# Layer 0's mix of a four-layer graph network: three passes over split operands in place of a recursive scheme of seven products

## The chip, the cores and the metric

The kernel runs on one core of a Trainium2 chip. The metric is the device time of one execution in microseconds (us); lower is better. A run reports the time of the whole execution; a profiled execution also reports the span from its first to its last recorded instruction, and the trace times every instruction within that span.

The engines of the core are TensorE (PE in the profile, with its weight loads listed apart as PEld), VectorE (DVE), ScalarE (ACT) and GpSimd (POOL). SyncE (SP) issues the DMAs. Matrix products are written by PE into PSUM, which is used in banks of 512 fp32 values for each of 128 partitions; the other engines read results from there.

## The reference

Input x has 32 batches of 512 nodes with 128 features; adj is a 512 x 512 matrix of non-negative weights. Four layers follow one another, each as x + layer(relu(layernorm(x))). Only layer 0 is changed:

```python
h0 = einsum('bnf,fg->bng', input, W[0])
h1 = einsum('bnf,fg->bng', input, W[1])
m = adj > 0
idx = cumsum(m.reshape(-1)) - 1
vals = e[0][idx].reshape(adj.shape)
A = softmax(where(m, vals, NEG), axis=1)
M = eye(N)
out = einsum('ij,bjg->big', A * M, h0) + einsum('ij,bjg->big', A * (1 - M), h1)
return out + bias
```

So each batch gets the off-diagonal attention times h1 (the mix, here written g), plus the diagonal of the attention times h0 (the own term), plus a bias. Layer 1 multiplies with adj and its square and projects with Theta; layer 2 passes messages through adj squared; layer 3 is an attention over the nodes. All inputs and outputs are fp32.

## The kernel before

**Tiling.** Nodes are cut into NT = 4 blocks of 128, batches into 16 pairs (index q, tiles of 128 x 4 x 2 x 128) and the pairs into 8 rounds of two (index r). All x stays on the chip from its load in layer 0 to its store at the end. A tile with nodes on the partitions serves the statistics and the mix; a projection needs features on the partitions, so each normalised tile h is turned into hT.

**Order.** PE, DVE, ACT and POOL run their instructions in the order in which the program writes them, and SP issues its DMAs in that order too. There is no scheduler: the order is written by hand with generators, where `next(steps)` emits the next part of a job and `go(steps, n)` its next n parts. Where an instruction waits, everything written behind it on the same engine waits as well.

**Start (up to L719).** The attention is made in four blocks of rows: exponentials, row sums, scaling by ACT (L677), then transposes by PE into the four banks `p_attT` (`transpose_rows`). ACT and DVE copy these banks into `attT` (`att_copies`, L346). `att_sums` (L348 to L366) lets DVE form three further sums s1, s2 and s4 of the four 256 x 256 quarters of attT. Meanwhile the first pairs are normalised, turned by PE (`pe_steps`, transposes in L307, for pairs 0 to 3) and projected.

**A pair before the mix.** `stats_steps` (L241 to L261) has DVE take BATCH_NORM_STATS2 over four stretches (L247), ACT the square root (L256), DVE a reciprocal (L258) and a shift `sh` (L259). `normed_steps` has ACT normalise with relu in eight instructions (L289). `turn_steps` (L320 to L335) turns a pair in two halves: DVE transposes blocks (L325), four DMAs write them to DRAM (L332) and one loads the turned tile (L334). `projected` (L458) multiplies by W[1] in 16 records of PE for a pair, `project_steps` (L472 to L484) has ACT copy the two banks to g (L483). `straight` (L733) lets POOL multiply hT with the attention's diagonal into hd, the left operand of the own term.

**The mix (`round0`, L804 to L958).** One round does two pairs by Strassen's scheme on 2 x 2 quarters: seven products in place of eight, in the order ORDER (L376 to L380). A left operand is a quarter of attT or a sum of quarters; a right operand is a part of g or one of four differences that POOL makes (`right_steps`, L368 to L374). `by_token` (L393 to L399, matmul in L397) does one product in four fp32 matmuls of 256 columns, each in two records. Products that share a result are accumulated in the banks a, c and d. `evict` (L824 to L844) has DVE add the banks into three tiles u or into x, and `add` (L850) has POOL add each u into x. The own term (`straight_block`, L801: four fp32 matmuls of 128 columns, eight records, for each call, four calls a round) is put in the banks as they end, and one bank of its own closes the round. The bias is added by POOL for the first quarter (`bias`, L466) and otherwise by the first eviction.

Between the products stand the other jobs of the round: turns of pairs 2r+2 and 2r+3, normalising two pairs on, statistics of pairs five ahead (`stats_a`, `stats_c`), statistics of the pairs whose layer 0 has ended (`own_a`, `own_c`, for layer 1), projections and right-hand differences of the next round, and the loads of x eight pairs on. From r = 3 on `late_parts` (L744 to L762) splits adj for layer 1. In round 0 the second half of the attention's transposes and copies stand inside the first products, and so do the transposes of adj for layer 1's square (`turn_adj`, L502 to L513).

**Layer 1** (from L960) is opened with `next(next_layer)` in the last round. Layers 1 to 3 use operands split in three parts (`PARTS`, high, low and mid; L424, L425) and matmuls of type fp32r for such products (`p_w`, L1010).

The order of the products, and the form of one:

```python
    ORDER = ((1, "a", True), (6, "c", True), (5, "d", True), (7, "c", False), (2, "a", False),
             (4, "c", False), (3, "d", False))
```

Of the kernel before, what the change touches and what calls it, by code (L numbers as in the profile page):

```python
# [17 lines left out]
P = 128  # L18
# [11 lines left out]
def kernel(  # L30
# [63 lines left out]
    def square_tile(name):  # L94
        return region0.tile([P, NT, N], F32, tag="square", name=name, bufs=2)
# [245 lines left out]
    sums = {}  # L341

    def att_copies(*which):

        for j, half, copy in which:
            copy(attT[:, j, half * H : half * H + H], pt[j][:, half * H : half * H + H])  # L346

    def att_sums():  # L348

        a11, a12 = attT[:, 0:2, 0:H], attT[:, 2:4, 0:H]  # L350
        a21, a22 = attT[:, 0:2, H:N], attT[:, 2:4, H:N]
        extra = region0.tile([P, 3, 2, H], F32, tag="sums", name="sums_att", bufs=1)
        s1, s2, s4 = extra[:, 0], extra[:, 1], extra[:, 2]
        sums["att"] = {1: a11, 2: a12, 3: s4, 4: a22, 5: s1, 6: s2, 7: a21}
        yield
        for out, p, bank_of, half, first in ((s1, a21, 2, 1, False), (s2, s1, 0, 0, False),
                                             (a21, a21, 0, 0, True), (s4, s2, 2, 0, True)):
            for k in range(2):
                b = pt[bank_of + k][:, half * H : half * H + H]
                if out is s1:  # L360
                    nc.vector.tensor_add(out[:, k], b, p[:, k])
                elif first:
                    nc.vector.tensor_sub(out[:, k], b, p[:, k])
                else:
                    nc.vector.tensor_sub(out[:, k], p[:, k], b)
            yield  # L366

    def right_steps(half, name, engs, right):  # L368
        b11, b12, b21, b22 = half(0, 0), half(0, 1), half(1, 0), half(1, 1)
        t = [region0.tile([P, 2, 2, D], F32, tag="rt", name=f"rt_{name}_{i}", bufs=6) for i in range(4)]  # L370
        right.update({1: b11, 2: b21, 3: b22, 4: t[3], 5: t[0], 6: t[1], 7: t[2]})
        for i, (p, q) in enumerate(((b12, b11), (b22, t[0]), (b22, b12), (b21, t[1]))):
            engs[i].tensor_sub(t[i], p, q)
            yield  # L374

    ORDER = ((1, "a", True), (6, "c", True), (5, "d", True), (7, "c", False), (2, "a", False),  # L376
             (4, "c", False), (3, "d", False))


    ORDER0 = (ORDER[0], ORDER[4]) + ORDER[1:4] + ORDER[5:]  # L380

    def products(name, form, left, right, evict, order=ORDER, on=lambda k, p: p):


        banks = {}
        for k, g, first in order:
            if first:
                banks[g] = bank(f"p_{name}_{g}")
            form(on(k, banks[g]), left[k], right[k], first)
            evict(k, banks[g])  # L390
            yield

    def by_token(p, a, b, first):  # L393

        for i in range(2):
            for k in range(2):
                nc.tensor.matmul(p[:, i * 2 * D : (i + 1) * 2 * D], a[:, k, blk(i)], b[:, k],  # L397
                                 start=(first and i == 0 and k == 0), stop=(k == 1),
                                 skip_group_check=True)  # L399

    def u_tile(name):
        return region0.tile([P, 2, H], F32, tag="u", name=f"u_{name}", bufs=3)
# [59 lines left out]
    def quad_tile(name):  # L462
        return region0.tile([P, 2, 2 * N], F32, tag="quad", name=name, bufs=2)


    def bias(r):  # L466
        x11 = xq[r][:, :, 0, 0:2, :]
        nc.gpsimd.tensor_add(x11, x11, b0[:, None, None, :].to_broadcast([P, 2, 2, D]))

    g, rights = {}, {}  # L470

    def project_steps(q, hT, copy=nc.scalar.copy):  # L472
        r, w = divmod(q, 2)
        if w == 0:
            if r % 3 == 2:
                g[r] = square_tile(f"g_{r}").rearrange("p t (b w f) -> p t b w f", b=2, w=2)
            else:
                t = quad_tile(f"g_{r}").rearrange("p w e -> p (w e)")
                g[r] = t.rearrange("p (t b w f) -> p t b w f", t=NT, b=2, w=2)
        pg = [projected(f"p_g_{q}_{b}", (at(hT, b), w0[:, 1, :])) for b in range(2)]  # L480
        yield
        for b in range(2):
            copy(g[r][:, :, b, w, :], pg[b])  # L483
            yield  # L484

    def right_of(r):
        rights[r] = {}
        return right_steps(lambda J, b: g[r][:, 2 * J : 2 * J + 2, b], f"g_{r}", [nc.gpsimd] * 4, rights[r])
# [84 lines left out]
    for i in range(3):  # L573
        eh = prep.tile([P, NK], BF16, name=f"eh_{i}")
        nc.gpsimd.tensor_copy(eh, ecoln)
        part = prep.tile([P, NK], F32, name=f"part_{i}")
        nc.gpsimd.tensor_copy(part, eh)
        if i < 2:
            nc.gpsimd.tensor_sub(ecoln, ecoln, part)
        parts.append(part)  # L580
    h = {q: normed_tile(q) for q in range(3)}
    hT = {q: feature_major(f"hT0_{q}") for q in range(4)}
# [26 lines left out]
    nc.vector.tensor_sub(rest, rows[:, :NK], pb[:, :, 0])  # L609
    def turn_first(b):  # L610
        p = bank(f"p_hT0_0_{b}")
        for t in range(NT):
            nc.tensor.transpose(p[:, blk(t)], h[0][:, b, t, :], ident)
        nc.scalar.copy(hT[0][:, :, b, :].rearrange("p b (a c) -> p b a c", c=QR), crossed(p))
# [10 lines left out]
    project = [project_steps(q, hT[q], c) for q, c in ((0, nc.scalar.copy), (1, nc.vector.tensor_copy))]  # L625
# [47 lines left out]
    def scaled_rows(t):  # L673
        if t == 0:
            nc.gpsimd.tensor_scalar(split(att[:, t, :]), crossed(us[t]), total[:, t : t + 1], None, OP.mult)
        else:
# [6 lines left out]
    attT = square_tile("attT")  # L683
# [4 lines left out]
    next(project[0])  # L688
# [10 lines left out]
    next(turned[1])  # L699
    scaled_rows(1)  # L700
# [5 lines left out]
    inverse(3)  # L706
    scaled_rows(3)
    next(project[1])
# [3 lines left out]
    go(project[1])  # L712
    left_of_att = att_sums()
    next(left_of_att)
    att_copies((0, 0, nc.scalar.copy), (1, 0, nc.vector.tensor_copy),
               (2, 0, nc.scalar.copy), (3, 0, nc.scalar.copy))
    go(early_stats_2, 3)
    next(squares)
    go(right_of(0))  # L719
# [59 lines left out]

    def projection(q):  # L780
        return project_steps(q, hT[f"hT0_{q}"] if q > 3 else hT[q])

    def diagonal_of(r, b):
        for q in (2 * r, 2 * r + 1):
            src = hT[f"hT0_{q}"] if q > 3 else hT[q]
            hd[q, b] = straight(src, b, adiag[0], f"hd_{q}_{b}")

    def x_block(r, I, b):
        return xq[r][:, :, b, 2 * I : 2 * I + 2, :]

    def of_pairs(ap):
        return ap.rearrange("p i (w f) -> p w i f", w=2)

    def halves(p):
        return p.rearrange("p (i e) -> p i e", i=2)

    def straight_block(p, src, I, weight, first):

        for i in range(2):
            for w in range(2):  # L800
                nc.tensor.matmul(p[:, (2 * i + w) * D : (2 * i + w + 1) * D], src(w)[:, blk(2 * I + i)], weight,  # L801
                                 start=(first and i == 0 and w == 0), stop=True, skip_group_check=True)

    def round0(r):  # L804

        now = rights.pop(r)
        if r == 0:

            adiag.append(region0.tile([P, N], F32, tag="rt", name="adiag", bufs=6))
            p_adiag = bank("p_adiag")
        A, C = 2 * r, 2 * r + 1

        def x_of(I, b):
            return x_block(r, I, b)

        def diagonal(p, I, b, first):
            straight_block(p, lambda w: hd[A + w, b], I, w0[:, 0, :], first)

        u = [u_tile(f"l0_{r}_{i}") for i in range(3)]
        held = {}

        def evict(k, p):  # L824
            pv = halves(p)
            if k == 1:
                nc.vector.tensor_add(tiles(u[0].rearrange("p i e -> p (i e)")), tiles(p), spread(b0, NT))
            elif k == 6:
                nc.vector.tensor_add(u[1], pv, u[0])
            elif k == 5:  # L830
                held["d"] = pv
            elif k == 7:
                nc.vector.tensor_add(u[2], pv, u[0])
                nc.vector.tensor_add(u[2], held["d"], u[2])
            elif k == 2 and r == 0:
                held["a"] = p
            elif k == 2:
                upper(p)
            elif k == 4:
                diagonal(p, 1, 0, False)  # L840
                nc.vector.tensor_add(x_of(1, 0), of_pairs(pv), x_of(1, 0))
            elif k == 3:
                diagonal(p, 0, 1, False)
                nc.vector.tensor_add(x_of(0, 1), of_pairs(pv), x_of(0, 1))  # L844
# [724 lines left out]
```

## Time and profile before

| what | value |
|---|---|
| median of 3 runs | 883.46 us (883.32 to 883.58) |
| profiled execution | 883.48 us |
| span of its trace | 881.7 us |
| instructions in the span | 15,654 |
| granted TensorE clock, 202.7 to 881.7 us | 1.00 |
| layer 0: first product starts | 28.96 us |
| layer 0: round 0 ends | 52.63 us |
| layer 0: rounds 1 to 6, each | 19.23 us |
| layer 0 ends, layer 1's first product follows | 183.6 us |
| PE busy from 202.7 to 881.7 us | 675.07 of 679.0 us |
| bytes moved by DMA | 102.81 MB |

How to read it: the times of day in the trace count from the start of the span. An engine's busy time leaves out issuing, branching and waiting on semaphores, but matmuls are pipelined with modelled ends, so a busy PE can hide short waits. The views used are the page's busy shares; the chain of waits, which follows the work that ended last back from step to step, each line with its start, its length, engine, tile and source line; the groups of instructions by line, with their count, mean duration and the idle time ahead of them; single instructions in a stretch of the timeline; and the windows, which give the busy time of each engine in a chosen stretch, with the count of its instructions behind it, then the granted clock, the DMAs' share and rate.

### The profile page before, as it was taken

The page shows a single profiled execution, that of the slowest core. Times are in us where ns is not written, and L with a number is a line of the kernel's source. Part 1 is how long each engine was busy: PE and PEld are TensorE (multiplying, and loading weights), DVE is VectorE, ACT ScalarE, POOL GpSimd, SP SyncE. Part 2 cuts the span into 40 slices and gives each one's busy share as a digit, 9 for nine tenths or more (in the row PEclk, how much of TensorE's full clock was granted, in tenths as well). Part 3 has the DMA queues.
Part 4 walks back from the last instruction along what each step waited for, and adds up shares of the span by engine and source line. Part 5 has one row for each costly group of instructions (what it writes and reads, how often), then busy time and mean ns, then how long its engine had stood idle before and what let it go on. Part 6 is the DMA issues. An engine that isn't in the chain of part 4 may idle for free.

```text
span 881.7 us, 15654 instructions
## 1 busy us (share of the span) xinstructions
PE 872.6 (99%) x5209; PEld 763.3 (87%) x5209; DVE 713.2 (81%) x1445; ACT 576.5 (65%) x1289; POOL 618.0 (70%) x599
## 2 busy tenths in 40 slices
PE   8999999999999999999999999999999999999998
PEld 4899999988888888888888888888889888899987
DVE  7888887568787787888689888888789789988875
ACT  5874554355556656556666888876688778766774
POOL 5876899986767877867586566565476766677664
PEclk9999999999999999999999999999999999999999
DMA  9166553131413113122242344455445555455433
GB/s 263 46 174 166 161 153 104 41 97 56 128 57 93 53 52 93 48 72 72 81 136 79 114 139 140 129 156 146 129 129 142 154 149 169 139 140 155 125 104 84
DMA packets 106960, 102.81 MB, mean 117 GB/s; under 512 B 9472, under 2 KB 93568, under 8 KB 106880
## 3 DMA queue, kind: packets, MB, share of 16 engines
q1 hardware_dynamic: 106592, 101.29, 41.0%
q8 instruction: 41, 0.67, 0.3%
q10 hardware_dynamic: 288, 0.52, 0.2%
q14 instruction: 39, 0.32, 0.1%
HBM read 52.50 MB, written 49.28 MB: 115 GB/s over the span
## 4 chain that ended last, share of the span: by engine, by line
PE 93%; POOL 3%; ACT 2%; DVE 1%; issue 1%; DMA 0%; POOLq 0%; ACTq 0%
PE p_av L1339 13%; PE p_l L1031 10%; PE p_hidden L1235 10%; PE p_score L1317 9%; PE p_x1T L409 9%; PE p_w L1010 5%; PE p_l_c L397 5%; PE p_l L458 3%; PE p_z L458 3%; PE p_l_a L397 3%; PE p_l_d L397 3%; PE p_g L458 3%; PE p_w L1012 3%; PE p_feat L1212 3%; PE p_hidden L1215 3%; PE p_query L1271 2%
## 5 line engine op out<-in xcount | busy, mean ns | idle before, releaser
L1339 PEld LDWEIGHTS p_av<-hv,ex 128*128 128x128 f32 x1024 | 119.1, 191 | 4.1 <-POOL hv L1301 1.1
L1339 PE MATMUL p_av<-hv,ex 128*128 128x129 f32 x1024 | 119.7, 274 | 0.8 <-POOL hv L1301 0.6
L289 ACT ACTIVATE h<-x,sh,rs 128x128 f32<-128x128 f32 x256 | 102.2, 483 | 11.9 <-DVE sh L259 11.0
L439 POOL TENSOR_TENSOR key<-key 128x512 fp32r<-128x512 f32 x32 | 48.1, 1503 | 83.9 <-DVE key L438 58.0
L1312 DVE TENSOR_TENSOR ex<-ex,adjTx 128x512 f32<-128x512 f32 x64 | 80.5, 1260 | 31.0 <-ACT ex L1310 29.2
L1312 POOL TENSOR_TENSOR ex<-ex,adjTx 128x512 f32<-128x512 f32 x64 | 99.6, 1573 | 6.9 <-issue 3.5
L1141 ACT ACTIVATE h<-x,sh,rs 128x128 f32<-128x128 f32 x256 | 102.9, 484 | 0.0
L247 DVE BATCH_NORM_STATS2 bn<-x 128x6 f32<-128x256 f32 x244 | 87.3, 417 | 0.0
L425 POOL TENSOR_TENSOR low_h<-h,high_h 128x512 fp32r<-128x512 f32 x32 | 54.5, 1704 | 45.9 <-PE p_w L1012 28.1
L1318 ACT ACTIVATE ex<-p_score 128x512 f32<-128x512 f32 x128 | 76.3, 598 | 11.5 <-PE p_score L1317 4.7
L1310 ACT ACTIVATE ex<-ex 128x512 f32<-128x512 f32 x128 | 77.3, 634 | 0.0
L1199 POOL TENSOR_SCALAR high_hT<-hT 128x512 fp32r<-128x512 f32 x32 | 20.5, 639 | 56.2 <-PE p_hidden L1215 28.8
L1255 POOL TENSOR_TENSOR x<-x,phi2b 128x256 f32<-128x256 f32 x64 | 56.2, 898 | 0.0
L425 POOL TENSOR_TENSOR low_hs<-hs,high_hs 128x512 fp32r<-128x512 f32 x32 | 44.4, 1399 | 13.2 <-ACT high_hs L424 12.9
L411 ACT COPY x1T<-p_x1T 128x512 f32<-128x512 f32 x32 | 18.7, 586 | 52.2 <-PE p_x1T L409 52.2
L1317 PE MATMUL p_score<-high_query,key 128*128 128x512 f32 x128 | 50.6, 395 | 0.0
L1317 PE MATMUL p_score<-low_query,key 128*128 128x512 f32 x128 | 50.5, 394 | 0.0
L1317 PE MATMUL p_score<-mid_query,key 128*128 128x512 f32 x128 | 50.4, 394 | 0.0
L443 ACT ACTIVATE high_query<-p_query 128x512 fp32r<-128x512 f32 x32 | 19.2, 601 | 47.5 <-PE p_query L1271 47.5
L256 ACT ACTIVATE sd<-bn,eps 128x8 f32<-128x8 f32 x46 | 14.0, 304 | 55.3 <-DVE bn L247 52.2
L1012 PE MATMUL p_w<-th,x1T 128*128 128x128 f32 x256 | 49.0, 272 | 0.0
L1150 DVE STREAM_TRANSPOSE hb<-h 128x512 f32<-128x512 f32 x64 | 43.6, 698 | 2.8 <-DMA d<-hb 2.6
(256 smaller groups left out, 2612.8 us busy)
## 6 DMA issues: line engine op xcount, KB each, us to landing
d<-hb SPq DMA_DIRECT2D x128, 128.0 KB, 2.4
hT<-d SPq DMA_DIRECT2D x32, 512.0 KB, 3.6
d_hT<-hb_hT SPq DMA_DIRECT2D x112, 128.0 KB, 2.4
hT<-d_hT SPq DMA_DIRECT2D x28, 512.0 KB, 3.3
x<-in_x_dram SPq DMA_DIRECT2D x32, 256.0 KB, 5.1
dv<-hvb SPq DMA_DIRECT2D x128, 64.0 KB, 1.9
hvt<-dv SPq DMA_DIRECT2D x32, 256.0 KB, 2.5
out_dram<-x SPq DMA_DIRECT2D x31, 256.0 KB, 2.5
```

The costliest lines, as they stand in the source:

```text
L247: nc.vector.bn_stats(st[:, k].rearrange("p e s -> p (e s)"), xt[q][:, b, t : t + 2, :].rearrange("p t f -> p f t"))
L289: nc.scalar.activation(h[:, b, t, :], xt[q][:, b, t, :], AF.Relu, bias=shift[q][:, i : i + 1], scale=scale[q][:, i : i + 1])
L397: nc.tensor.matmul(p[:, i * 2 * D : (i + 1) * 2 * D], a[:, k, blk(i)], b[:, k], start=(first and i == 0 and k == 0), stop=(k == 1), skip_g ...
L409: nc.tensor.matmul(p, right[part][:, blk(t)], left[part][:, t, :], start=(t == 0 and part == 0), stop=(t == NT - 1 and part == 2))
L425: nc.gpsimd.tensor_sub(low, x, high.bitcast(F32))
L458: nc.tensor.matmul(p[:, blk(t)], hT(t), w, start=(i == 0), stop=(i == len(terms) - 1))
L1031: nc.tensor.matmul(p, adj_parts[part][:, t, blk(i)], w[r][part][:, t, :], start=(part == 0 and t == 0), stop=(part == 2 and t == NT - 1))
L1141: nc.scalar.activation(h[:, t, :], xt[q][:, b, t, :], AF.Relu, bias=shift[q][:, i : i + 1], scale=scale[q][:, i : i + 1])
L1235: nc.tensor.matmul(sums2[n], weighed_features[n][i][:, blk(t)], sq[i][:, t, :], start=False, stop=(i == 2 and t == NT - 1), skip_group_che ...
L1312: eng.tensor_mul(split(ex[:, t, :]), split(ex[:, t, :]), crossed(mask[:, t, :]))
L1317: nc.tensor.matmul(p, keys[n][i][:, t, :], query[n][i], start=(i == 0), stop=(i == 2))
L1339: nc.tensor.matmul(po[:, i, : D + 1], ex[:, t, blk(i0 + i)], hv[:, t, :], start=(t == 0), stop=(t == NT - 1))
```

## The change

The recursive scheme goes, and with it the sums of the attention's quarters, the right-hand differences, the tiles u and the rounds of two pairs. In its place:

- The transposed attention is split from its PSUM banks into three fp32r tiles `att_high`, `att_low` and `att_mid`, in two halves: four scaled high parts, on ACT (for the first half two of them on DVE), then four low and four mid parts on DVE. There is no fp32 `attT`.
- g of each pair is split as it leaves PSUM: ACT makes the high part by a scaled copy, DVE the low part from the bank and the high part, POOL the mid part from the two. W[1] is scaled beforehand by a power of two, on POOL. For pair 0 `project_first` does it by way of a copy in SBUF, so that the banks come free.
- The mix of a pair is three passes (high, low, mid), each over two halves of the nodes: `mixed` makes one pass of one half with eight fp32r matmuls of 256 columns. The three passes accumulate in one bank for each half.
- The own term of a pair goes into the same two banks, ahead of the passes (for pair 0 behind them). One addition on DVE for each bank then brings it into x.
- The bias is added by POOL to the whole of x, two instructions a pair.
- The loop runs over single pairs, 1 to 15. A pair's order in it: own term, turn of pair q+3, normalising of q+4, statistics of q-1 for layer 1, projection and split of q+1, three passes of half 0, statistics of q+5, addition, three passes of half 1, addition.
- Pair 3 is turned by DVE and DMAs, not by PE. The transposes of adj move from the start to pairs 3 and 4, their DMAs to pair 5; the split of adj runs one part a pair from pair 6 on; layer 1 is opened in pair 14, and its next part stands in pair 15.

The core of the diff:

```diff
-        return region0.tile([P, NT, N], F32, tag="square", name=name, bufs=2)
+        return region0.tile([P, NT, N], F32, tag="square", name=name, bufs=1)
...
-    def att_sums():
...
-    def right_steps(half, name, engs, right):
...
-    def products(name, form, left, right, evict, order=ORDER, on=lambda k, p: p):
...
-    def by_token(p, a, b, first):
...
+    att_parts = [region0.tile([P, NT, N], F32R, name=f"att_{part}", bufs=1) for part in PARTS]
...
+    def att_high(j, half, on_act):
+
+        p, (high, low, mid) = of_half(j, half)
+        if on_act:
+            nc.scalar.activation(high, p, AF.Copy, scale=DOWN)
+        else:
+            nc.vector.tensor_scalar(high, p, DOWN, None, OP.mult)
+
+    def att_low(half):
+
+        for j in range(NT):
+            p, (high, low, mid) = of_half(j, half)
+            nc.vector.tensor_sub(low, p, high.bitcast(F32))
+
+    def att_mid(half):
+
+        for j in range(NT):
+            p, (high, low, mid) = of_half(j, half)
+            nc.vector.scalar_tensor_tensor(mid, p, 1.0 / UP, high.bitcast(F32), OP.mult, OP.subtract)
...
+    def bias(q):
+
+        for b in range(2):
+            nc.gpsimd.tensor_add(xt[q][:, b], xt[q][:, b], spread(b0, NT))
...
         pg = [projected(f"p_g_{q}_{b}", (at(hT, b), w0[:, 1, :])) for b in range(2)]
         yield
+        g_tiles(q)
         for b in range(2):
-            copy(g[r][:, :, b, w, :], pg[b])
+            high, low, mid = (part[:, :, b, :] for part in g[q])
+            nc.scalar.activation(high, pg[b], AF.Copy, scale=DOWN / LOW)
             yield
...
+            nc.vector.scalar_tensor_tensor(low, high.bitcast(F32), -LOW, pg[b], OP.mult, OP.add)
+            nc.gpsimd.tensor_sub(mid, high.bitcast(F32), low.bitcast(F32))
+            yield
...
+    nc.gpsimd.tensor_scalar(w0[:, 1, :], w0[:, 1, :], LOW * UP, 1.0, OP.mult, OP.mult)
...
-    go(project[1])
-    left_of_att = att_sums()
-    next(left_of_att)
-    att_copies((0, 0, nc.scalar.copy), (1, 0, nc.vector.tensor_copy),
-               (2, 0, nc.scalar.copy), (3, 0, nc.scalar.copy))
+    for j in range(NT):
+        att_high(j, 0, j % 2 == 0)
+    att_low(0)
+    att_mid(0)
     go(early_stats_2, 3)
-    next(squares)
-    go(right_of(0))
+    next(project[1])
+    next(project[1])
+    next(project[1])
...
+    def own_sums(q, ps, first):
...
+                    nc.tensor.matmul(p[:, (2 * i + b) * D : (2 * i + b + 1) * D], hd[q, b][:, blk(2 * I + i)], w0[:, 0, :],
+                                     start=(first and i == 0 and b == 0), stop=not first, skip_group_check=True)
+
+    def mixed(q, I, p, part, first):
 
         for i in range(2):
...
+            for t in range(NT):
+                nc.tensor.matmul(p[:, i * 2 * D : (i + 1) * 2 * D], att_parts[part][:, t, blk(2 * I + i)],
+                                 g[q][part][:, t].rearrange("p b f -> p (b f)"),
+                                 start=(first and part == 0 and i == 0 and t == 0), stop=(part == 2 and t == NT - 1),
+                                 skip_group_check=True)
+
+    def added(q, I, p):
+
+        x = xt[q][:, :, 2 * I : 2 * I + 2, :].rearrange("p b i f -> p i b f")
+        nc.vector.tensor_add(x, p.rearrange("p (i b f) -> p i b f", i=2, b=2), x)
+
+    def first_sums():
...
+        ps = opened_sums(0)
+        mixed(0, 0, ps[0], 0, True)
+        transpose_rows(pt, att, 2)
+        transpose_rows(pt, att, 3)
+        go(early_stats_2)
+        go(normal[2], NT)
+        for j in range(NT):
+            att_high(j, 1, True)
+        att_low(1)
+        att_mid(1)
+        mixed(0, 0, ps[0], 1, True)
+        mixed(0, 0, ps[0], 2, True)
...
+        diagonal_of(0, 0)
+        diagonal_of(0, 1)
+        go(ln3, NT + 1)
+        go(normal[2])
+        go(ln3)
+        mixed(0, 1, ps[1], 0, True)
+        mixed(0, 1, ps[1], 1, True)
+        mixed(0, 1, ps[1], 2, True)
+        next(turned[2])
+        normalise(3)
+        diagonal_of(1, 0)
+        diagonal_of(1, 1)
+        go(turned[2])
+        go(project[1])
+        go(ahead[4], NT + 1)
+        own_sums(0, ps, False)
+        go(turn(3))
+        go(ahead[4])
+        bias(0)
+        for I in range(2):
+            added(0, I, ps[I])
+        own[0] = stats_steps(0)
+
+    def round0(q):
...
+        ps = opened_sums(q)
+        own_sums(q, ps, True)
+        if q == 1:
+            normalise(4)
+            go(ahead[5])
+        elif q + 3 < NQ:
+            go(turn(q + 3))
...
+        if q > 1:
+            go(normal_of, NT)
+        go(own[q - 1], NT + 1)
+        if q == NQ - 1:
+            next(next_layer)
+        if more:
+            diagonal_of(q + 1, 0)
+            diagonal_of(q + 1, 1)
+            steps = projection(q + 1)
+            next(steps)
+            bias(q + 1)
+            go(steps)
+        go(own[q - 1])
+        if q == 1:
+            go(turn(4))
+        go(normal_of)
+        if q >= 6:
+            go(sums_ahead, 1)
+        for part in range(3):
+            mixed(q, 0, ps[0], part, False)
+        go(stats_of, NT + 1)
+        added(q, 0, ps[0])
+        go(stats_of)
+        if q in (3, 4):
+            next(squares)
+            next(squares)
+        if q == 5:
+            go(squares)
+        for part in range(3):
+            mixed(q, 1, ps[1], part, False)
+        added(q, 1, ps[1])
+        own[q] = stats_steps(q)
+        if q % 2 and q // 2 + NQ // 4 < NQ // 2:
+            loads(q // 2 + NQ // 4)
...
+    first_sums()
+    bias(1)
+    for q in range(1, NQ):
+        if q == NQ - 2:
             next(next_layer)
-        round0(r)
+        round0(q)
```

## The prediction

> **What bounds the kernel now.** I read the page's busy shares first, then the chain of waits, then the busy time of each engine in windows one round of layer 0 long (a round is four batches), then single stretches of the timeline.
>
> ```profile
> PE 872.6 (99%) x5209; PEld 763.3 (87%) x5209; DVE 713.2 (81%) x1445; ACT 576.5 (65%) x1289; POOL 618.0 (70%) x599
> ```
> TensorE is busy 99% of the 881.7 us. A busy PE in this view can still be a waiting one, so the chain has to confirm it:
>
> ```profile
> 52.80 1.73 PE p_l_a L397 x8
> 54.53 1.73 PE p_l_c L397 x8
> 56.25 1.73 PE p_l_d L397 x8
> 57.98 1.78 PE p_g L458 x16
> ...
> 72.03 1.73 PE p_l_a L397 x8
> ```
> The chain runs through PE without a gap, and the same product comes back after 19.23 us in every round. One product (four fp32 matmuls of 256 columns, eight records) takes 1.73 us, one projection 1.78. The windows of two rounds show what the others do meanwhile:
>
> ```profile
> 52.80:72.03 19.23, 19.23 (x121) 17.79 (x121) 16.89 (x39) 10.02 (x26) 14.88 (x13) 1.00 0.60 177
> 91.26:110.50 19.24, 19.24 (x122) 17.79 (x121) 16.87 (x37) 10.56 (x26) 17.38 (x15) 1.00 0.59 168
> ```
> The columns after the length are PE, PEld, DVE, ACT, POOL. The granted clock is 1.00. PE is full, but DVE has 16.87 of 19.23 and POOL up to 17.38: there are only 2 us of room a round under PE.
>
> **PE's work in the steady rounds.** Before, a round has 7 products x 1.73 = 12.11, two projections 3.57, and own products (L801) 4 x 8 records x 0.111 = 3.56: 19.24, as measured. After, a round is one pair of batches, so two make one old round. Each pair has 3 passes x 16 matmuls = 48 fp32r matmuls of 256 columns. The trace has that form in layer 1 (L1010, three in a row, each with its own weight load):
>
> ```profile
> 203.39 0.35 PE p_w L1010 x3
> 203.75 0.22 PE p_w L1012 x2
> ```
> 0.35 for three is 0.117 each: 48 x 0.117 = 5.60. With own products 1.78 and a projection 1.785 a pair costs 9.17 of PE, two cost 18.34: **0.90 us less** for each old round, 7.2 over eight. PE's transposes of pair 3 go too (eight records of 0.11, 0.9 us; DVE and the DMAs take them). So PE has some 8.1 us less to do in all.
>
> The Trainium skill speaks against this part: "TensorE: Matmul & The Clock Gate" (section LDWEIGHTS) gives a weight load of 128 columns 128/1.2 = 107 ns, and says in "What overlaps and what doesn't" that it overlaps a running matmul only in another row group. The passes raise the weight loads of the mix from 448 to 768; 320 loads more at 107 ns would, as an estimate by that page, add 34 us. L1010 above has load and matmul in 0.117 together, so here the loads are hidden.
>
> **What DVE, POOL and ACT get.** Per two pairs the counts hardly move. DVE: eight evictions of 512 columns before (L827 to L952, 0.69 each); after, four additions into x and four low parts, each with one PSUM operand too. POOL: 4 hd + 4 right-hand sums + 3 additions + 1 bias = 12 tensor operations of 1.27; after, 4 hd + 4 bias + 4 mid = 12. ACT: four copies of 0.58 become four scaled copies. What is new is a chain inside a pair. DVE's order is: transposes, four statistics of the pair before, the two low parts, their reciprocal and shift, four statistics ahead, addition, shift, addition. ACT takes the square root of those statistics before the high parts, so DVE, having ended the statistics, waits for square root and high part:
>
> ```profile
> 95.87 2.73 DVE L247 BATCH_NORM_STATS2 bn<-x 128x6 f32<-128x256 f32 x8
> 97.36 0.30 ACT L256 ACTIVATE sd<-bn,eps 128x8 f32<-128x8 f32 x1 [1.81 <-DVE bn L247]
> 98.69 0.30 ACT L256 ACTIVATE sd<-bn,eps 128x8 f32<-128x8 f32 x1 [1.02 <-DVE rs L258]
> 98.90 1.05 ACT L483 COPY g<-p_g 128x512 f32<-128x512 f32 x2
> ```
> After the fourth statistic (97.28) the root starts 0.08 later, the next ACT instruction 0.21 after a root, and a copy of 512 takes 0.58; with 0.05 to wake DVE that is some 0.9 us in which DVE stands. Nothing else is put there. DVE's pair is then 16.87/2 + 0.9 = **9.3 us against PE's 9.17**. What moves this most is the shift (L259), which both orders have twice a pair:
>
> ```profile
> L259 DVE SCALAR_TENSOR_TENSOR sh<-bn,rs x23: 166/975/1085, 54.7 to 174.4; 128x8 f32<-128x8 f32 x23
> ```
> It needs 0.17 alone and mostly takes 0.98, because it stands behind a POOL operation. If POOL's phase lets half of that go, the pair is 9.1; if root and high part come later by a few ACT instructions, 9.6. I take 9.3. It applies while statistics run ahead (pairs 3 to 11); later pairs have 2.4 us less of DVE. POOL: 6 x 1.24 + 1.25 (the split of adj, one a pair from 6 on) = 8.7 of 9.17, which holds.
>
> **The start** is where the change pays. Before, the first product follows the transposes at once:
>
> ```profile
> 27.33 1.32 ACT L677 ACTIVATE att<-u,total 128x512 f32<-128x512 f32 x2
> 28.56 0.90 ACT L346 COPY attT<-p_attT 128x256 f32<-128x256 f32 x3
> 28.96 1.99 PE L397 MATMUL p_l_a<-g,attT 128*128 128x256 f32 x8 [0.29 <-ACT attT L346]
> ```
> After, I follow the new order with the durations of the same engines' rows:
> - ACT: two high parts of pair 0 (1.16, as L424's pairs) stand before the scaling of rows 1; the next exponential absorbs 0.3 of it. Rows 2 and 3 are scaled at 29.4 instead of 28.65, and ACT's high parts of att end at 30.0.
> - DVE: g's low parts 28.3 to 29.6, two high parts of att to 30.3, four low (0.33 each) to 31.65, four mid to 33.0. PE does pass high at 30.3 to 31.2 and then waits: the transposes of rows 2 and 3 write banks that att_mid still reads. They end at 33.2; passes low and mid and the diagonal's broadcast at 36.1.
> - DVE's second half of pair 2's statistics stands behind all that: 33.7. ACT's root 34.05, high parts of pair 1 to 35.0; DVE's low part, reciprocal, shift to 35.8; ACT normalises half of pair 2 (1.65) to 37.5 and only then makes the second half of att's high parts, to 38.6. DVE's low to 39.05, mid to 40.45; PE's three passes of the lower half end at 41.1.
> - Pair 3's statistics 41.8, root 42.15, the rest of pair 2's normalising 43.7, its transposes on PE 43.9; own products of pair 0 to 45.7 and of pair 1 to 47.45; projection of pair 2 to 49.25, the passes of pair 1 to **54.85**.
> Before, PE had pairs 0 and 1 done at 52.63, with pair 3's projection (1.785) done too: the start costs 54.85 - 52.63 + 1.785 = **4.0 us**, PE's smaller work already in it.
>
> **Sum for layer 0.** From 54.85 PE needs 14 pairs x 9.17 less one projection: 126.6, so 181.45. Before, its last own product ends at 183.6. To add: pair 4's transposes end on DVE at 58.75 and a turned tile lands some 7.3 us later (a pair of L325 ended at 66.1, its load was issued at 70.0 and takes 3.3), so at 66.1; PE wants it at 65.8: 0.3 (up to 2.3 if the load is issued 5.9 after, as the pair that ended at 56.9 had it, behind loads of x). The transposes of adj (4 x 0.64 on DVE) move from the start to pairs 3 and 4, where DVE is now nearly full: pair 6's mid part then comes 1.6 us after PE wants it (at 9.3 a pair; 0.5 at 9.1, 2.8 at 9.6). Pairs 7 to 12 lose 0.13 each, 0.8. End of layer 0: 181.45 + 0.3 + 1.6 + 0.8 = 184.15, **0.55 later** than before. adj's four writes (3.4 us of SP) move behind pair 8's turn; pair 9's turn has a pair's time of slack, so they cost nothing; without that, at most the 3.4.
>
> In layer 1 POOL's first low part stands behind th's low part, which now waits for the second of pair 15's last three passes (0.93 before the end) and takes 0.73; with 1.28 to 1.7 (L425) the low part is there 1.1 to 1.5 after layer 0's end, and PE wants it 0.93 after: 0.3 (0 to 0.8). From there PE was full, and a delay passes to the end. 0.55 + 0.3 = 0.85. The profiled execution took 883.48 (span 881.7, 1.8 around it), the median is 883.46. 883.48 + 0.85: **forecast 884.3.**
>
> Costed at nothing: the scaling of w0 on POOL (0.2, the nearest row L235) delays pair 1's shift, but ACT idles 0.7 before the first exponential; uncovered, 0.2. The smaller pools cost no instruction.
>
> **Rivals.**
> - *PE's saving survives.* If DVE's pair stays under 9.17 and the start costs 1.5 us less than walked (each of six hand-overs between DVE and ACT is an estimate good to 0.25), layer 0 ends at 181.45 + 0.3 - 1.5 = 180.25, 3.35 earlier; with 0.3 in layer 1: 880.4. For it: all counts are equal and PE saves 8.1 in all. Against: DVE's 16.87.
> - *DVE becomes the loop* (slower). Place: the wait of the low part for root and high part, nine pairs. It decides from 9.3 on. At 9.6: 181.45 + 0.3 + 2.8 + 6 x 0.43 = 187.1, 3.5 later; with 0.5 in layer 1: 887.5. For it: shifts at 0.98 and the median of L259; against: the low parts have a PSUM operand, and such instructions keep 0.69 beside POOL (L829, L833).
> - *The passes are not 0.117.* 48 in a row with other weights have no row; bounds are 0.111 (L801's records, own loads) and 0.122 (half of p_l's 0.233 plus 5%): 16 x 48 x 0.006 = -4.6 to +3.8. I stay at 0.117, the same form.
>
> **Numbers.** One measurement tells 0.2% (1.77 us) from no change. Forecast's case (layer 0's loss and gain cancel to within 1.7 us): 0.38. PE's saving survives, or the passes run at 0.111, beyond -0.2%: 0.23. DVE's loop, a start longer than walked, or passes at 0.122, beyond +0.2%: 0.39. The range takes in both ends of the passes' price, 884.3 - 4.6 = 879.7, and above the loop together with a start 1.5 us longer, 887.5 + 1.5 = 889.0.
>
> **What would show it.** Right: L0's passes at 0.93 per eight; gaps of PE between 29 and 44 with DVE or ACT as releaser; between pairs 5 and 12 waits of PE for low or mid parts of under 0.5 each; the first x1T of layer 1 within 2 us of 183.6. Wrong: no gap of PE in the rounds (then DVE's pair is shorter), a start that ends its pair 1 more than 1.5 us from 54.85, or passes above 0.12.

## The result and the profile after

| | before | after |
|---|---|---|
| median | 883.52 us (883.32 to 884.4) | 896.02 us (891.87 to 897.8) |
| ratio to before | | 1.0133, 95% interval 1.0093 to 1.0173 |
| profiled execution, span | 883.48, 881.7 | 897.80, 896.0 |
| pair 1's passes end (before: round 0 ends) | 52.63 | 56.70 |
| layer 0's last matmul ends | 183.6 | 190.0 |
| layer 1's first x1T starts | 183.61 | 194.96 |
| from there to the span's end | 698.1 | 701.1 |

The change made the kernel slower by some 12.5 us, and less regular: its four executions lie 6 us apart, those of the kernel before 1 us. The page's first part hardly tells it:

```profile
PE 875.4 (98%) x5520; PEld 773.6 (86%) x5521; DVE 730.2 (81%) x1453; ACT 576.4 (64%) x1291; POOL 619.6 (69%) x600
```
PE has 2.8 us more of busy time in a span 14.3 us longer; DVE has 17 us more, and that is the trace of the cause: 14.2 us of them are in one group, the shift (L259; 34.1 us in all layers before, 48.3 after), which has no new work. The group up to 200 us, before and after:

```profile
L259 DVE SCALAR_TENSOR_TENSOR sh<-bn,rs x27: 166/957/1085, 33.5 to 174.4; 128x8 f32<-128x8 f32 x27
L259 DVE SCALAR_TENSOR_TENSOR sh<-bn,rs x29: 166/631/8486, 36.2 to 190.7; 128x8 f32<-128x8 f32 x29
```
The three durations are the shortest, the median and the longest. The median is shorter than before (631 ns against 957), but the longest is 8.49 us for an instruction that needs 0.17 alone. The timeline of POOL and DVE, with one line of ACT, around another such shift, of 8.22 us (start, length, engine, line; in brackets what the engine waited for):

```profile
129.19 2.55 POOL L429 TENSOR_TENSOR x<-x,b 128x512 f32<-128x512 f32 x2
131.71 2.51 POOL L447 TENSOR_TENSOR g_mid<-g_high,g_low 128x512 fp32r<-128x512 f32 x2
132.24 8.22 DVE L259 SCALAR_TENSOR_TENSOR sh<-bn,rs 128x8 f32<-128x8 f32 x1
134.19 1.26 POOL L731 TENSOR_TENSOR adj_s<-adj_s,adj_high 128x512 f32<-128x512 f32 x1
135.42 2.51 POOL L714 TENSOR_TENSOR hd<-hT,adiag 128x512 f32<-128x512 f32 x2
137.89 2.54 POOL L429 TENSOR_TENSOR x<-x,b 128x512 f32<-128x512 f32 x2
140.39 1.43 DVE L247 BATCH_NORM_STATS2 bn<-x 128x6 f32<-128x256 f32 x4
141.91 0.31 ACT L256 ACTIVATE sd<-bn,eps 128x8 f32<-128x8 f32 x1 [8.60 <-DVE bn L247]
```
POOL's seven operations from 131.71 on stand end to end, and the shift ends 0.03 us after the last of them (140.46 against 140.43). Then DVE goes on, and ACT, which stood 8.60 us for DVE's statistics, makes that root, normalises, waits 1.52 us for the next statistics, and only behind a second root starts g's high part, at 146.14. PE meets this one pair later:

```profile
143.75 1.95 PE L422 MATMUL p_g<-w,hT 128*128 128x128 f32 x16
147.26 1.21 PE L786 MATMUL p_l<-g_high,att_high 128*128 128x256 f32 x8 [1.56 <-ACT g_high L444]
148.31 1.12 PE L786 MATMUL p_l<-g_low,att_low 128*128 128x256 f32 x8
150.10 1.22 PE L786 MATMUL p_l<-g_mid,att_mid 128*128 128x256 f32 x8 [0.67 <-POOL g_mid L447]
```
The windows of pairs show the same as busy time (PE, PEld, DVE, ACT, POOL, clock, DMA share and rate): a plain pair, the pair of the long shift, and the one after it.

```profile
56.70:66.03 9.33, 9.33 (x83) 9.33 (x82) 8.35 (x20) 6.30 (x16) 7.51 (x7) 1.00 0.23 58
132.64:141.97 9.33, 9.33 (x83) 9.33 (x82) 9.33 (x6) 0.73 (x3) 7.79 (x7) 1.00 0.19 57
141.97:154.04 12.07, 9.84 (x83) 9.45 (x81) 10.78 (x27) 8.63 (x21) 6.35 (x8) 1.00 0.31 88
```
In the second, DVE is "busy" all 9.33 us with six instructions: a busy DVE can be a waiting one. The shift of 8.49 us runs from 178.4 to 186.9, at the end of layer 0. Behind it stand the additions into x and the statistics of layer 1's first pairs, and PE waits 4.8 us before layer 1:

```profile
189.04 1.12 PE L786 MATMUL p_l<-g_mid,att_mid 128*128 128x256 f32 x8
194.96 2.07 PE L373 MATMUL p_x1T<-adj_high,high_h 128*128 128x512 f32 x4 [4.80 <-ACT high_h L388]
196.94 2.07 PE L373 MATMUL p_x1T<-adj_low,low_h 128*128 128x512 f32 x4
```
Four such matmuls take 1.09 later and 2.07 here. The windows say why: between 195 and 200.5 the clock (third number from the end) is 0.54.

```profile
190.00:195.00 5.00, 0.20 (x3) 0.05 (x1) 2.13 (x7) 4.17 (x12) 1.26 (x2) 0.82 0.42 105
195.00:200.50 5.50, 5.50 (x13) 3.96 (x14) 4.24 (x5) 4.02 (x10) 5.38 (x4) 0.54 0.46 98
200.50:210.00 9.50, 9.50 (x60) 8.45 (x60) 3.40 (x7) 5.20 (x12) 6.15 (x7) 1.00 0.31 112
```
The trace's record of the clock has it at half from 193.24 to 200.07; the 5.1 us of that in which PE worked cost 2.55.

**Where the profiled execution lost time against the prediction's steps** (13.5 us in all: its span is 14.3 us longer than before, and 0.85 of that was forecast); a pair's time is read from the start of one pair's own products to the next's:

| step | predicted | measured | more |
|---|---|---|---|
| pair 1's passes end | 54.85 | 56.70 | +1.85 |
| 14 pairs less a projection | 126.6 (9.17 a pair) | 128.8 (9.325 a pair) | +2.2 |
| pair 4's turned tile | 0.3 | 10.50 - 9.33 = 1.17 | +0.9 |
| adj's transposes on DVE, and pairs 7 to 12 | 1.6 + 0.8 | 9.47 - 9.33 = 0.14 | -2.3 |
| held shift of 8.22 | none | (12.07 - 9.33) + (9.77 - 9.33) = 3.18 | +3.2 |
| layer 0's end | 184.15 | 190.0 | +5.85 |
| from there to the first x1T | 0.3 | 4.96 | +4.7 |
| from the first x1T to the end | 698.1 | 701.1 | +3.0 |

### The profile page after: what moved, and what is told of

It reads as the page before. It is cut to its first block, busy times and chain, and to the rows that moved or that the text cites. A ratio compares the mean times of both kernels' runs of the same rounds, so it can differ in the third digit from the quotient of the medians.

```text
span 896.0 us, 16275 instructions
## 1 busy us (share of the span) xinstructions
PE 875.4 (98%) x5520; PEld 773.6 (86%) x5521; DVE 730.2 (81%) x1453; ACT 576.4 (64%) x1291; POOL 619.6 (69%) x600
## 4 chain that ended last, share of the span: by engine, by line
PE 78%; POOL 9%; DVE 5%; issue 3%; ACT 3%; DMA 1%; SPq 0%; POOLq 0%; ACTq 0%; DVEq 0%
PE p_av L1270 12%; PE p_l L962 10%; PE p_hidden L1166 10%; PE p_score L1248 9%; PE p_x1T L373 9%; PE p_w L941 5%; PE p_l L422 3%; PE p_z L422 3%; PE p_w L943 3%; PE p_feat L1143 2%; PE p_hidden L1146 2%; PE p_query L1202 2%; PE p_hv L1214 2%; PE p_l L786 2%; POOL g_mid L447 2%
## 5 line engine op out<-in xcount | busy, mean ns | idle before, releaser
L447 POOL TENSOR_TENSOR g_mid<-g_high,g_low 128x512 fp32r<-128x512 f32 x30 | 37.6, 1273 | 20.0 <-DVE g_low L446 19.9
L259 DVE SCALAR_TENSOR_TENSOR sh<-bn,rs 128x8 f32<-128x8 f32 x61 | 48.3, 793 | 2.1
```

## The experiments

**Theory A**: DVE's shift reads two operands from SBUF and is held while POOL works without a pause. **Theory B**: DVE stands at these places for another reason. **Theory C**: the stalls set nothing, and the start and the dearer passes explain the time.

**The changed kernel again.** No edit.

> The changed kernel itself, once more, to see how its time varies. Its first profile took 897.8 us and held two shifts (sh, L259) of 8.22 and 8.49 us on DVE, each ending 0.02 us after a chain of POOL operations that stood end to end. Theory A: DVE's shift reads both operands from SBUF and is held while POOL runs without a break; whether it slips in between two POOL operations is chance, so the number of long shifts varies from run to run and the time with it: 887 to 889 without one, 892 to 898 with one or two. Theory B: DVE stands at these places for a reason of its own (its instructions come late, say): the same two stalls at the same two pairs in every run, 897 to 898, and a spread below 1 us.

Measured: 897.2 us median of six, 892.07 to 899.2. The profile has the two long shifts at the same places, 8.22 at 132.15 and 8.33 at 178.47. So Theory A's "chance" was wrong for these places, as far as profiles show, and B was right about them; the spread of 7 us speaks for A. Of the ten executions of this kernel six lie between 897 and 899.2, three at about 892 and one at 894.35; what the faster ones lacked is not shown, because both profiles are of executions above 897.

**The shift on POOL.**

```diff
-        nc.vector.scalar_tensor_tensor(sh, st[:, :, :, 1], -1.0, rs, OP.mult, OP.mult)
+        if on is nc.vector:
+            nc.vector.scalar_tensor_tensor(sh, st[:, :, :, 1], -1.0, rs, OP.mult, OP.mult)
+        else:
+            nc.gpsimd.tensor_scalar(sh, st[:, :, :, 1], -1.0, None, OP.mult)
+            nc.gpsimd.tensor_mul(sh, sh, rs)
...
-        own[q] = stats_steps(q)
+        own[q] = stats_steps(q, on=nc.gpsimd)
```


> Layer 0's shifts are made by POOL in two small operations (0.24 and 0.21 us by the rows of L276 and L278) in place of one on DVE. Theory A: no DVE instruction of layer 0 over 1.5 us, PE's waits of 2.7 us near 146 and of 4.8 us before layer 1 go, and with them the half clock of 6.8 us that follows the second: 897.8 - 3.2 - 4.6 - 2.5 = 887.5 us, and executions within 1 us of each other. Theory B: DVE still stands some 8 us at two places, 892 to 898. Theory C: the stalls do not set the end, and the time stays with the start and the dearer passes: 894 to 898 without any stall on DVE.

Measured: 891.35 us, 890.99 to 892.45. No hold, every pair from 3 on 9.33, and the first x1T at 187.44, near the 187.2 that 194.96 less the expected 3.2 and 4.6 gives: A and not B or C. But 4 us of the expected gain did not come: from the first x1T to the end it took 702.9 us against 701.1 after and 698.1 before. An opening of layer 1 that had hidden behind the long wait came to light: PE waits 1.47 us at a p_w for a low part (of hs), and half a clock from 199.11 to 202.52 follows. SP's part of the timeline names the origin (first two lines: the kernel before; then this one, with PE's wait last):

```profile
177.95 2.96 SPq L332 DMA_DIRECT2D d_hT<-hb_hT  x4
182.91 0.34 SPq L334 DMA_DIRECT2D hT<-d_hT  x1
183.10 7.93 SPq L336 DMA_DIRECT2D d_hT<-hb_hT  x5
191.25 0.34 SPq L338 DMA_DIRECT2D hT<-d_hT  x1
191.64 1.40 SPq L336 DMA_DIRECT2D d_hT<-hb_hT  x3
198.63 0.38 PE L945 MATMUL p_w<-th_high,low_hs 128*128 128x256 f32 x1 [1.47 <-POOL low_hs L393]
```
Five writes stand ahead of the first load, not four: the fifth belongs to layer 1's pair 1 and waits for DVE's transposes, which end at 190.7. So the load of pair 0 goes out at 191.25 instead of some 3 us earlier (before, it went out 4.96 behind the start of the first write). Before, the order on SP was four writes, the load, four writes. In the changed kernel SP has the new order too. The prediction had looked at POOL alone here.

**Openings on POOL.** A memset of one column, which reads nothing, behind each mid part and each hd.

```diff
             nc.gpsimd.tensor_sub(mid, high.bitcast(F32), low.bitcast(F32))
+            opening()
...
+    def opening():
+        nc.gpsimd.memset(gap_cell, 0.0)
...
         nc.gpsimd.tensor_mul(split(s), hT[:, :, b, :].rearrange("p b (a c) -> p a b c", c=QR), split(scale))
+        opening()
```


> POOL gets a one-column memset (0.10 us by the rows of such memsets) after each mid part of g and each hd, which reads nothing from SBUF: four a pair, 0.4 us of POOL. Theory A: the held shift gets in there, no sh over 1.4 us: 887 to 888.5 us. If POOL keeps its interfaces even for an instruction that only writes: shifts of several us as in the changed kernel, 892 to 898. Theory B: two stalls as before, 896 to 898.

Measured: 897.56 us, 894.9 to 898.06, with shifts of 8.42 and 8.72 us. The start of the chain around the first:

```profile
131.52 1.33 POOL L447 TENSOR_TENSOR g_mid<-g_high,g_low 128x512 fp32r<-128x512 f32 x1
132.03 8.42 DVE L259 SCALAR_TENSOR_TENSOR sh<-bn,rs 128x8 f32<-128x8 f32 x1
132.74 0.14 POOL L452 MEMSET gap_cell<- 128x1 f32 x1
132.79 1.31 POOL L447 TENSOR_TENSOR g_mid<-g_high,g_low 128x512 fp32r<-128x512 f32 x1
134.00 0.14 POOL L452 MEMSET gap_cell<- 128x1 f32 x1
```
The shift that began at 132.03 got in at none of the four memsets that stand in its time. So such a memset is no pause for the shift. Whether that is because POOL keeps the shift out while it only writes is not shown: in the trace the next operation starts 0.05 us after a memset does, so the opening may have been too short.

**No bias.** Layer 0's bias is left out, so that POOL must pause in each pair.

```diff
     def bias(q):
...
-        for b in range(2):
-            nc.gpsimd.tensor_add(xt[q][:, b], xt[q][:, b], spread(b0, NT))
+        pass
```


> The bias of layer 0 is left out (two POOL operations of 1.25 us a pair), so that POOL has 5 to 6.2 us of work in a pair of 9.3 and must pause in each. Theory A: a shift waits for the rest of a short chain at most, under 4 us, and PE does not see it: 886.5 to 888 us. Theory B: as before, 896 to 898.

Measured: 889.53 us, 888.38 to 890.62; the longest shift is 1.23 and the first x1T stands at 185.55. A again: with pauses on POOL there is no hold. The time is 1.5 us above the range: from the first x1T to the end it took 703.2, with the same wait of 1.47 and the same five writes ahead of the load as with the shift on POOL.

**Layer 1's opening and the start.** Three kernels with POOL's shifts for pairs 4 on. The first has the load of layer 1's pair 0 issued by ACT, the second another order in the start, the third both:

```diff
+        if name == "hT1_0":
+            yield
+        load = nc.scalar if name == "hT1_0" else nc.sync
...
+        turn(0)
         normalised(2)
...
-        go(normal[2], NT)
         for j in range(NT):
             att_high(j, 1, True)
+        go(normal[2], NT)
...
-        go(ln3, NT + 1)
         go(normal[2])
```


> Shifts of pairs 4 on and of layer 1's pairs by POOL as in the kernel with the shift on POOL (pairs 2 and 3 keep DVE's), and the load of layer 1's first turned pair issued by ACT behind the high parts, not by SP, where it stood behind a write of the second pair that waits for DVE until 190.7. If that order is what holds layer 1 up: hs of pair 0 at 192 and not 195.4, no wait of PE of 1.47 us at the first p_w and no half clock behind it: first x1T at 186.5 to 187, 698.5 us from there on as in the kernel before, 886.5 to 888 us. If layer 1's opening is held by POOL's work (low parts) instead: 1 us less than the 891.35 of the kernel with the shift on POOL, from the start alone.

> The same shifts by POOL; the load by SP as in the changed kernel; in the start ACT makes att's second high parts ahead of the normalising of half of pair 2, which waits for a shift, and the second half of that normalising ahead of pair 3's square root. If ACT's order lengthens the start: PE's wait of 0.9 to 2.4 us near 38 goes, the passes of pair 1 end at 54 to 55 (56.1 to 57.3 before), 888 to 889.5 us with layer 1's opening as it was. If DVE's splitting of att is what the start lasts: no gain, 890 to 891.

> Both edits. If both theories hold they add up: first x1T at 184.5 to 185.5, 884 to 886 us, near the kernel before. If a new wait takes the place of one of them: 887 to 889.

Measured: 887.84 (887.75 to 888.3), 887.49 (887.03 to 889.01) and 884.97 us (884.86 to 885.42). With the load by ACT, hs of pair 0 starts at 192.01 and not 195.45, the wait of 1.47 is gone, and from x1T to the end it takes 699.0. With the new order the first x1T stands at 184.1 against 187.1, and PE's wait near 38 for att's second high parts is gone. The second kernel came a little better than expected (888 to 889.5), with 701.2 from x1T to the end: the wait of 1.47 is still there, but no half clock behind it. The load by ACT is worth 2.5 us (second against third), the order of the start 2.9 (first against third), and both add up: the two theories hold. The third kernel is 1.0015 of the time before (1.0007 to 1.0024).

**The shift's second operand from PSUM.** The strictest test of A: the shift keeps its engine and its place, POOL its chain; only where one operand lies is changed. One of the eight banks is given to it.

```diff
         nc.vector.reciprocal(rs, sd)
-        nc.vector.scalar_tensor_tensor(sh, st[:, :, :, 1], -1.0, rs, OP.mult, OP.mult)
+        cell = cell_bank[:, 0, q]
+        nc.vector.reciprocal(cell, sd)
+        nc.vector.scalar_tensor_tensor(sh, st[:, :, :, 1], -1.0, cell, OP.mult, OP.mult)
```


> The changed kernel, with DVE's shifts where they were, but their second operand read from PSUM: the reciprocal is made a second time into a PSUM bank kept for it (seven banks remain for all layers, which may cost a few us in any layer; so the shifts are what is read, not the time). If the shift is held because it reads two operands from SBUF: every sh at 0.2 to 0.4 us, none near 1 or 8, and the first x1T at 187 to 188. If one operand in SBUF, the result or DVE's place in the order is enough to hold it: shifts of 0.6 to 1.3 us as before and the two of over 8 us.

Measured: 889.54 us, 889.1 to 889.97, and of the shifts in all layers:

```profile
L263 DVE SCALAR_TENSOR_TENSOR sh<-bn,cell_bank x61: 161/163/167, 37.4 to 637.5; 128x8 f32<-128x8 f32 x61
```
All 61 took 0.161 to 0.167, and 50 of them overlap an operation of POOL; in the kernels before and after, that time was only met where no operation of POOL ran or where one ended during the shift. Layer 0 shows no wait of PE after 41 us: every pair from 2 on takes 9.33, pair 4's tile is in time, and the first x1T is at 185.93, over 1 us earlier than expected. So it is the second operand in SBUF that lets POOL hold DVE. The rest of the time above the kernel before stands elsewhere: 701.7 us from x1T to the end, with the wait of 1.47 for the late load.

**More of the start.** On the third kernel above (shifts of pairs 4 on by POOL) five further moves in the start.

```diff
     next(project[1])
+    go(early_stats_2)
     next(project[1])
...
         mixed(0, 0, ps[0], 0, True)
+        mixed(0, 0, ps[0], 1, True)
         transpose_rows(pt, att, 2)
         transpose_rows(pt, att, 3)
-        go(early_stats_2)
...
-        go(normal[2], NT)
         att_low(1)
         att_mid(1)
-        mixed(0, 0, ps[0], 1, True)
...
         mixed(0, 1, ps[1], 2, True)
+        own_sums(0, ps, False)
         next(turned[2])
...
-        own_sums(0, ps, False)
         go(turn(3))
         go(ahead[4])
+        diagonal_of(2, 0)
+        diagonal_of(2, 1)
         bias(0)
...
```


> On the kernel with both edits: pair 2's shift stands ahead of g's low part (so that it is not held by POOL's mid part, 1.24 us near 35.5), the low pass ahead of the transposes of att's rows 2 and 3 (it fills PE's wait of 0.9 us near 31.4), the copy of the diagonal ahead of pair 2's normalising, the own products of pair 0 ahead of pair 2's transposes, and hd of pair 2 ahead of the biases of pairs 0 and 1 (PE waits 0.48 and 0.73 us for it near 54). If the start is a chain over DVE and POOL as the waits show it: 1.8 us by the passes of pair 1 and 1.2 us behind them, 881.5 to 883 us, faster than the kernel before. If the waits only move (DVE's eight splittings of att's second half end no earlier): 884 to 885.

Measured: 884.99 us (884.52 to 886.26), the second case: pair 1's passes end at 52.4 instead of 53.5, and PE gives it back at once (the profile is of the longest execution, 886.26).

```profile
56.91 1.22 PE L794 MATMUL p_l<-g_high,att_high 128*128 128x256 f32 x8 [0.79 <-ACT g_high L451]
59.76 1.21 PE L794 MATMUL p_l<-g_mid,att_mid 128*128 128x256 f32 x8 [0.67 <-POOL g_mid L454]
66.32 2.02 PE L429 MATMUL p_g<-w,hT 128*128 128x128 f32 x16 [0.60 <-DVE g_low L453]
76.85 1.35 PE L429 MATMUL p_g<-w,hT 128*128 128x128 f32 x10 [0.98 <-DMA hT<-d_hT]
```
PE comes earlier than the pairs are normalised, split and turned.

**The two halves of a bank in turn**, for the pace of the passes.

```diff
-        for i in range(2):
-            for t in range(NT):
+        for t in range(NT):
+            for i in range(2):
```


> The kernel with both edits, its passes in another order: the two halves of a bank in turn, so that no matmul adds to the columns that the one before it wrote. If that is what makes a matmul of a pass start 0.120 us after the last and not 0.117: 0.110 to 0.117, and a pair of PE 0.15 to 0.5 us shorter. If the pace is that of loading and streaming alone: 0.120, and the time of the kernel with both edits, 885.

Measured: 884.77 us in one execution; from one matmul's start to the next's it is 120 ns as before, and a pair 9.33. So the 0.120 does not come from writing the same columns in a row.

**What could be had together.** The shift from PSUM with the load by ACT and the order of the start, and the same with the five further moves.

> The shift's second operand from PSUM in place of shifts on POOL, with the load by ACT and the start order of the kernel with both edits. Theory: the shift's hold, the late load and ACT's order in the start were the three waits, and POOL without the shifts has hd of pair 2 ready, so that PE's 1.1 us near 54 go: 884.97 - 1.1 + 0.5 for seven banks = 884.4, in 883.6 to 885, and executions within 1 us of each other. If seven banks cost more: 885 to 887.

> The same with the fuller reordering of the start, which with shifts on POOL only moved PE's waits behind pair 1 (0.79 for g's high part, 0.67 for its mid part, 0.6 and 1.0 for turned pairs). If those came from the late shifts on POOL: 1.5 to 3 us less than the kernel before it in this call, 881.5 to 883. If the turns of pairs 3 and 4 (7 us each from DVE to landing) are what the start lasts: within 0.7 us of it, 883.5 to 885.

Measured: 884.45 (883.38 to 885.15, so not within 1 us of each other) and 886.66 us (885.63 to 887.51). The first is 1.0006 of the time before, 0.9997 to 1.0015: no difference that can be told. Its layer 0 ends 0.4 us earlier than before (first x1T 183.18), and the layers behind give it back: 700.1 from x1T to the end against 698.1, of which 0.35 is the first low part and 0.87 a wait of PE at a p_feat for a part of hT made by POOL; the rest is not shown. The profiles of the two other kernels with seven banks have no wait there, so the missing bank is not shown to be its cause. The second speaks against the theory that the shifts on POOL had made the new waits of the start: those at the high and the mid part are gone, but PE waits 1.08 us at 57.01 at a p_g for DVE's low part, and 0.70 at 66.40 for a turned tile. Its time is above both expected ranges, and why is open. No version beat the kernel before.

## Why the prediction was wrong

- **The failing step** is the sentence on POOL: "6 x 1.24 + 1.25 (the split of adj, one a pair from 6 on) = 8.7 of 9.17, which holds." The sum was near (8.44 in the window of such a pair). But it asked whether POOL gets its work done, and not what an almost unbroken POOL does to DVE, which was put at nothing. The prediction took the shift as standing "behind a POOL operation", 0.98, as the trace of before had it; the dearest case of its range was 0.98 at every shift. At two places where POOL ran seven operations end to end, a shift stood 8.22 and 8.49 us (up to 8.72 with the memsets). That cost 3.2 us in the rounds, 4.7 ahead of layer 1 and 2.55 of half clock behind it: 10.4 of the 13.5. The PSUM, no-bias and shift-on-POOL kernels each take one condition away, and each takes the hold away.
- The prediction's slower rival put DVE as the loop, with 9.6 a pair. It was not: away from the holds DVE is busy 7.8 to 8.6 of a pair, PE sets 9.33 with no gap, which the prediction had named as a sign that DVE's pair is shorter, and the shifts are shorter than before. DVE's wait for root and high part, put at 0.9, was 0.92. The rival had the right sign by luck, with the wrong mechanism.
- **The pass** was mis-sized: 0.117 from three matmuls of L1010 in a row, 0.120 in a stream of 48 (eight start at 138.12, the next eight at 139.08). The third rival had priced it up to 0.122; it costs 14 x 48 x 0.0033 = 2.2 us of the expected 7.2.
- **The start**: its waits came where they were put (att's mid part at 32, att's second high parts at 39, pair 2's normalised half at 43), and its end was 1.85 us late (the prediction's own sign of being wrong was 1.5). Pair 2's shift, begun at 36.17, took 1.25 behind POOL's mid part and ended at 37.42, where 35.8 had been put; ACT's normalising, att's high parts, and the low and mid parts follow it. The clock was at half from 32.81 to 36.23, but that is not the cause: in the changed kernel's second profile, without it, the first pass to pair 1's end took 26.41 us, against 26.43.
- **adj's transposes** and the rounds behind them cost 0.14 and not 2.4, and the 0.14 stands at pair 8; the pairs beside the transposes take 9.33. They had been priced against a DVE with no room.
- **Layer 1's opening**: 0.3 was predicted, and with holds and openings undone 0.35 was measured at the first low part. What was missed was a fixed order on SP, worth 2.5 us between the two kernels that differ in it alone.
- What the prediction cited from the Trainium skill, "TensorE: Matmul & The Clock Gate", on weight loads would, as an estimate, have put 34 us on the passes; the prediction was right not to follow it: the 768 loads are hidden here, at 120 ns for load and matmul together.

## What to carry to other kernels

Before loading POOL near to full, look for instructions on DVE that read two operands from SBUF, however small: behind an unbroken chain on POOL their cost can be the rest of the chain, not one operation. Read a duration far above its group's minimum as a wait, and ask what ended with it. And where a long wait goes, look at the queue of each engine, SP's too, for what stood behind it.

## What the runs showed of the hardware

- **A hold longer than one operation.** The Trainium skill, "SBUF — State Buffer" (section "Who interferes with whom"), says that a DVE instruction with two SBUF inputs contends with a GpSimd instruction that reads SBUF, and not with one that only writes. The operand in PSUM agrees with the first half (0.16 us always). The page's section "SBUF: two separate sides" has the lock held for one whole instruction and the other side blocked for it; here one shift was blocked over seven in a row (8.22 us). The memsets, which only write, let nothing in (8.42 and 8.72), but they stand between operations that read, with 0.05 us to the next, and so do not decide about the second half. What lets most shifts in at the first boundary of two POOL operations (four at the second, which began up to 0.12 us ahead of the first) and keeps two of 29 out until POOL stops was not found: the same pairs of operations stand on both sides of it.
- **A wait of PE can cost twice.** With a wait of 4.8 us the clock was at half for 6.83 us, in all three profiles that had such a wait (4.64, 4.80 and 5.03). For shorter waits the length alone does not decide: the same wait of 1.47 us at layer 1's first p_w was followed by 3.41 us of half clock with the shift on POOL (199.11 to 202.52) and without bias (196.90 to 200.31), and by none with the start's order alone and with the operand in PSUM; 2.44 us at 37 was followed by 6.83 with the shift on POOL, 1.96 there by none in the changed kernel's second profile.
- fp32r matmuls of 256 columns with a weight load each: 120 ns from start to start in a long stream, whether or not they add to the columns just written.
